# A recurrent attention layer with a sign-weight feed-forward part on one core: signs loaded in eight parts and the last block's loads in text order, two sums of products made by transfers, and zeros multiplied ahead of the first input

## The chip, the cores and the metric

The kernel runs on one core of a Trainium2 chip. A core has engines that run beside each other and meet through semaphores: PE (TensorE, matrix products; its weight loads, PEld, overlap the products), DVE (VectorE), ACT (ScalarE), POOL (GpSimd) and SP (SyncE). [...] Each engine takes its instructions in order.

The metric is the device time of one execution, in microseconds (us). Before the change it is 1445.28 us, the median of three runs (1454.41, 1443.0 and 1445.28).

## The reference

One layer over 2048 tokens of width 512, in float32. `_causal_dwconv` is a convolution of each channel over four tokens; `_lag(u, s)` is u moved by s tokens.

```python
xn = _layernorm(x)
# attention part: 16 heads of 128 channels, four lags
q = _silu(xn @ Wq); k = _silu(xn @ Wk); v = _silu(xn @ Wv); z = xn @ Wz
a = xn @ Wa; b = xn @ Wb
q, k, v = [_causal_dwconv(u, w) for u, w in ...]
q = q * cos + rot_half(q) * sin          # k the same way
q = q / max(norm(q), 1e-12)              # k the same way
for s in range(4):
    attn = einsum('bshd,bshd->bsh', q, _lag(k, s)) * scale
    gate = _sigmoid(_lag(a, s) * b)
    out = out + (attn * gate)[..., None] * _lag(v, s)
out = out * rsqrt(mean(out * out) + eps) * norm_w * _silu(z)
s = out @ Wout
# feed-forward part, with the signs of the weights
hidden = relu((xn @ sign(up_weight).T) * up_scale)
g = _silu((hidden @ sign(down_weight).T) * down_scale * output_scale)
result = x + s * g
```

## The kernel before

The 2048 tokens go in four blocks of 512 (b = 0 to 3), the 16 heads in eight pairs (p = 0 to 7), 256 channels each. Activations lie with channels on the 128 partitions and tokens along the free axis; `xnT` is the normalised input in this form. Products of float32 operands take two passes on PE, so a 128x512 product with four 128-row slices of weights shows up as eight PE instructions; a projection of one pair (two halves) is 16.

All PE and DVE instructions go through a small wrapper, `InOrder` (lines 68 to 78), which pins them to the order of the program's text. That is why the profile gives line 76 for nearly all of them; one tells them apart by tile. Instructions of ACT, POOL and SP are not wrapped: a scheduler places them, and their queues then run strictly in the order that it chose. A transfer that waits for a free buffer therefore holds up everything behind it on its queue.

*The start.* `first_layer_norm` (from line 144) loads the first 512 tokens in four chunks, takes their statistics on DVE and normalises them in place. `transpose` (168) turns each chunk on PE into a PSUM tile `tp`, which ACT copies into `xnT`. Then the first projection, `pq`, can start.

*The stage ahead of the blocks* (the loop with `step(p, -1, ...)`). For block 0 it makes q and k of each pair: projection, SiLU on ACT, convolution on DVE (`convolve`), rotation (`turn`), and in `products` (324) the products of q with the four lags of k, in two halves of 128 channels: tiles `pr` and `pr1`, 128x2048 each. The two are added; in block 0 DVE does that (line 361), in the other blocks, for even p, POOL issues an accumulating transfer (line 359). `sum_dots` later sums over the channels of a head by products on PE (`dots`). Beside this, the stage makes the feed-forward part of block 0 and writes the signs of the up and down weights to DRAM (`signs_dram`). Near its end, `gate_products(1)` sends four slices of gate products to DRAM: a plain transfer (227) and three accumulating ones (229), each of which waits for the one before it. They are on POOL's queue.

*The main loop.* For b = 0 to 2, `step(p, b)` makes v, the lag sums and the output of block b, and q, k of block b + 1. At p = 0 the sums of the block are turned into coefficients (`norms`, `norms_in_rows`, `coefficients`), which go to DRAM as `co_dram` and come back spread over partitions as `bc` (line 490): two tiles per pair, two transfers each, three buffers. `weighted` multiplies them with the lags of v (tiles `te`, `o`) on DVE; `gated_output` makes `oz`; `output_projection` (tile `po`) runs for two pairs at a time, and its results are added up in DRAM.

*The last block* has a loop of its own (line 736 on), with p one ahead of the output. It projects v (`pv`, weights `wv`) and z (`pz`, weights `wz`), all weights of v and z sharing three buffers with the tag `w` (`load`, line 246). Into memory that the first part no longer needs, POOL loads the signs of the up weights, `up` (4 MB), in four parts at p = 0 to 3, and `first_down` (1 MB) at p = 4. The loads of v are issued one p ahead. `raw`, `v`, `z` and `o` have one buffer each there.

*The feed-forward part of blocks 1 to 3* is a stream of up and down products on PE (`ph`, `pf`), with the hidden tiles of f split into two terms on DVE (`hid_hi`, `hid_lo`). In the last block the down products of the last four f are kept back and made by column chunk (0 and 1, then 2, then 3), so that DVE can finish one chunk (scale, SiLU on ACT, times y, plus x) while PE makes the next:

```python
if b == last and f >= NFC - 2:
    continue
_, df, terms = hids.pop(0)
```

The loop over f runs to NFC + 1, two past the last up product, and each turn takes one hidden tile, so this condition keeps four back.

Of the kernel before, what the change touches and what calls it, by code (L numbers as in the profile page):

```python
# [38 lines left out]
F32 = mybir.dt.float32  # L39
F32R = mybir.dt.float32r  # L40
AF = mybir.ActivationFunctionType
ALU = mybir.AluOpType
PSUM = bass.MemoryType.PSUM

P = 128
# [5 lines left out]
HALO = LAGS - 1  # L51
CH = H * D
KC = HID // P
NP = H // 2
TB = 512
# [5 lines left out]
NFC = FF // P  # L61
# [20 lines left out]
def recurrent_layer(ctx: ExitStack, tc: tile.TileContext, a: dict, out: bass.AP):  # L82
    nc = tc.nc
    pe, dve = InOrder(tc, nc.tensor), InOrder(tc, nc.vector)

    const = ctx.enter_context(tc.tile_pool(name="const", bufs=1))
    xnT = const.tile([P, KC, HALO + S], F32, name="xnT")
    ss_acc = const.tile([P, NT], F32, name="ss_acc")
# [76 lines left out]
        normalise(TC - 1)  # L165
        return x_in

    def transpose(x_in):
        for c in range(TC):
            tp = mm.tile([P, KC, P], F32, tag="mm", name=f"tp{c}")  # L170
            for k in range(KC):
                pe.transpose(tp[:, k, :], x_in[:, c, k * P : (k + 1) * P], ident)
            nc.scalar.copy(xnT[:, :, HALO + c * P : HALO + (c + 1) * P], tp)  # L173

    means = {}
# [68 lines left out]
    weights = {}  # L244

    def load(pool, n, p, b):
        w = pool.tile([P, KC, 2 * P], F32, tag="w", name=f"w{n}{p}_{b}", bufs=3)
        nc.sync.dma_start(w, a[f"w{n}"][p])
        weights[n] = w

    def with_halo(pool, name, tag, bufs, p, b):
# [22 lines left out]
    def raw_of(pool, n, p, b, bufs=2):  # L274

        raw = with_halo(pool, f"r{n}", "raw", bufs, p, b)
        project(n, p, b, raw[:, :, HALO:])
        keep_halo(f"r{n}", raw, p, b)
        return raw
# [44 lines left out]
    def products(p, b, q, between=None, beside_k=None):  # L324

        n = f"_{p}_{b}"
        load(qks, "k", p, b)
        q0 = q[:, LAGS - 1]
        k = with_halo(qks, "k", "k", 1, p, b)
        raw = raw_of(qks, "k", p, b)  # L330
        if p % 2 == 0:
            sum_squares()
        convolve(1, p, raw, k[:, :, HALO:])
        keep_halo("k", k, p, b)
        if between:
            between()
        turn(q)
        if beside_k:
            beside_k()

        sq = [qks.tile([P, 2, TB], F32, tag=f"sq{j}", name=f"sq{j}" + n, bufs=2 - j) for j in range(2)]
        for j in range(2):
            nc.scalar.activation(sq[j][:, 0], q0[:, j], AF.Square)
            nc.scalar.activation(sq[j][:, 1], k[:, j, HALO:], AF.Square)
        nc.gpsimd.dma_start(sq[0], sq[1], accum_op=ALU.add)
        squares_due.append((p, sq[0]))
        def product(to, j, lo, hi):

            k0 = k[:, j, lo : lo + TB]
            k_lags = bass.AP(k0.tensor, k0.offset, [k0.ap[0], [1, hi - lo], k0.ap[1]])  # L350
            dve.tensor_tensor(to, q[:, lo:hi, j, :], k_lags, ALU.mult)

        pr = qks.tile([P, LAGS, TB], F32, tag="pr", name="pr0" + n, bufs=2)
        product(pr, 0, 0, LAGS)
        if not b or p % 2 == 0:
            pr1 = qks.tile([P, LAGS, TB], F32, tag="pr", name="pr1" + n, bufs=2)
            product(pr1, 1, 0, LAGS)
            if b:
                nc.gpsimd.dma_start(pr, pr1, accum_op=ALU.add)
            else:  # L360
                dve.tensor_tensor(pr, pr, pr1, ALU.add)
        else:
            for lo in range(0, LAGS, 2):
                half = qks.tile([P, 2, TB], F32, tag="half", name=f"half{lo}" + n, bufs=1)
                product(half, 1, lo, lo + 2)
                dve.tensor_tensor(pr[:, lo : lo + 2], pr[:, lo : lo + 2], half, ALU.add)
        if not b:
            dots_due.append([p, pr, of_head[:, p], p == NP - 1, True])
            return


        for h in range(0, P, D // 2):
            first, second = slice(h, h + D // 4), slice(h + D // 4, h + D // 2)
            if p % 2 == 0:
                nc.gpsimd.dma_start(pr[first], pr[second], accum_op=ALU.add)
            else:
                both = dots_due[-1][1]
                nc.gpsimd.dma_start(both[second], pr[first])
                nc.gpsimd.dma_start(both[second], pr[second], accum_op=ALU.add)
        if p % 2 == 0:  # L380
            dots_due.append([p, pr, of_heads[:, p // 2], p == NP - 2, False])
        else:
            dots_due[-1][-1] = True
# [35 lines left out]
    squares = {}  # L419
# [40 lines left out]
    def values(p, b, raw):  # L460

        v = with_halo(vs, "v", "v", 1, p, b)
        convolve(2, p, raw, v[:, :, HALO:])
        keep_halo("v", v, p, b)
        return v
# [14 lines left out]
    def weighted(p, b, v):  # L480

        n = f"_{p}_{b}"
        o = vs.tile([P, 2, TB], F32, tag="o", name="o" + n, bufs=1)
        for s in range(LAGS):
            if s % 2 == 0:

                bc = vs.tile([P, 2, TB], F32, tag="bc", name=f"bc{s}" + n, bufs=3)
                for h in range(2):
                    row = co_dram[b][s : s + 2, 2 * p + h, :]
                    nc.sync.dma_start(  # L490
                        bc[h * D // 2 : (h + 1) * D // 2], row.partition_broadcast(D // 2)
                    )
            b2 = bc[:, s % 2].unsqueeze(1).to_broadcast([P, 2, TB])
            v_s = v[:, :, HALO - s : HALO - s + TB]
            if s == 0:
                dve.tensor_tensor(o, v_s, b2, ALU.mult)
            else:
                te = vs.tile([P, 2, TB], F32, tag="te", name=f"te{s}" + n, bufs=2)
                dve.tensor_tensor(te, v_s, b2, ALU.mult)
                dve.tensor_tensor(o, o, te, ALU.add)  # L500

        if p == 0:
            squares[b] = vs.tile([P, 2, TB], F32, tag="ss", name=f"ss{b}", bufs=1)
            nc.scalar.activation(squares[b], o, AF.Square)
        else:
            o2 = vs.tile([P, 2, TB], F32, tag="o2", name="o2" + n, bufs=1)
            nc.scalar.activation(o2, o, AF.Square)
            nc.gpsimd.dma_start(squares[b], o2, accum_op=ALU.add)
        return o

    def gated_output(p, b, o, z, wo):
# [47 lines left out]
    def step(p, b, beside_q=None, beside_k=None):  # L559
# [41 lines left out]
        if b + 2 < NTB:  # L601
# [4 lines left out]
            elif p == 5:  # L606
                divide(b + 2)

    x_in = first_layer_norm()
    small_loads()  # L610
    transpose(x_in)
    def in_two_terms(pool, x, tag, bufs, shape, name):
        hi = pool.tile(shape, F32R, tag=f"{tag}_hi", name=f"{name}_hi", bufs=bufs)
        lo = pool.tile(shape, F32R, tag=f"{tag}_lo", name=f"{name}_lo", bufs=bufs)
        dve.tensor_copy(hi, x)
        dve.tensor_tensor(lo, x, hi, ALU.subtract)
        return hi, lo
# [4 lines left out]
    def up_projection(ph, pool, f, b, up_f, xs):  # L622
        for k in range(KC):
            for i, term in enumerate(xs):
                pe.matmul(
                    ph,
                    up_f[:, k, :],
                    term[:, k, :],
                    start=(k == 0 and i == 0),
                    stop=(k == KC - 1 and i == 1),  # L630
                )
        hid = pool.tile([P, TB], F32, tag="hid", name=f"hid{f}_{b}", bufs=3)
        nc.scalar.activation(hid, ph, AF.Relu, scale=up_scale[:, f : f + 1])  # L633
        return in_two_terms(pool, hid, "hid", 4, [P, TB], f"hid{f}_{b}")


    G = 4
# [65 lines left out]
            step(p, b)  # L703

    last = NTB - 1
    load(vs, "v", 0, last)
    raw = raw_of(vs, "v", 0, last, 1)
    load(vs, "v", 1, last)
# [14 lines left out]
    NFD = 4  # L723
# [9 lines left out]
        return up[:, f].rearrange("p (k m) -> p k m", k=KC)  # L733


    for p in range(NP + 1):
        if 1 < p < NP:
            raw = raw_of(vs, "v", p, last, 1)
        if p:
            z, wo = gates_of_output(p - 1, last, zs)  # L740
        if p % 2 == 1:
            output_projections()
        if p < NP - 1 and p != 1:
            load(vs, "v", max(p + 1, 2), last)
        if 0 < p < NP:
            zs = weights_of_output(p, last)
            v = values(p, last, raw)
        if p:
            gated_output(p - 1, last, o, z, wo)
        if p < NP:  # L750
            o = weighted(p, last, v)
        if p < NFC // G:
            some = slice(G * p, G * p + G)
            nc.gpsimd.dma_start(up[:, some], signs_dram["up"][:, some])
        elif p == NFC // G:
            nc.gpsimd.dma_start(first_down, signs_dram["down"][:, 0:NFD])
        if p == 4:
            xs = in_two_terms(ffw, tokens(1), "xs", 1, [P, KC, TB], "xs1")
    hids = []
# [10 lines left out]
    with tc.tile_pool(name="ff", bufs=1, side="right") as ff, tc.tile_pool(  # L770
# [48 lines left out]
        for b in range(1, NTB):  # L819
            pf = [pfs.tile([P, HID], F32, name=f"pf{c}") for c in range(TC)]  # L820
            for f in range(2, NFC + 2):
# [13 lines left out]
                if f == NFC - 4 and b + 1 < NTB:  # L835
                    ahead = in_two_terms(
                        ff if b == 1 else ffw, tokens(b + 1), "xs", 1, [P, KC, TB], f"xs{b + 1}"
                    )
                if b == last and f >= NFC - 2:
                    continue  # L840
                _, df, terms = hids.pop(0)
                for c in range(TC):
# [87 lines left out]
```

## Time and profile before

The profile is of one execution, which took 1442.18 us, 1440.4 us of it the span between its first and its last instruction. The granted clock of PE was 0.99 on the mean.

| engine | busy, us | share of the span | instructions |
|---|---|---|---|
| PE (products) | 1401.4 | 97% | 3936 |
| PEld (weight loads) | 685.1 | 48% | 3936 |
| DVE | 1211.9 | 84% | 1363 |
| ACT | 612.9 | 43% | 1181 |
| POOL | 228.8 | 16% | 313 |

| transfers | packets | MB | share of 16 engines |
|---|---|---|---|
| issued by POOL (software queue) | 32512 | 104.89 | 38.0% |
| issued by SP (hardware queue) | 68624 | 153.53 | 36.4% |

The stages, by time from the start of the span: input and transposes until 11 us, the stage ahead of the blocks until about 210, the blocks 0 to 2 until about 1080, the last block until about 1256, the feed-forward part of the other blocks to the end. In a row of groups, waits or the timeline, "<-" between tiles reads "made from", and what stands after an idle time is who ended it. Lines such as L245 or L490 are lines of the kernel before; L76 is the wrapper.

### The profile page before, as it was taken

The numbers are of one execution on the slowest core, as the hardware profiler recorded it, in microseconds if no ns is written. First come the engines' busy times: TensorE is split into PE (matmuls) and PEld (weight loads), VectorE is DVE, ScalarE is ACT, GpSimd is POOL, SyncE is SP. The second block draws the span as 40 slices with busy tenths as digits, with TensorE's granted clock in tenths as the row PEclk, the third lists the DMA queues.
The fourth block names the chain that finished last, engine by engine and source line by source line (L and its number), as shares of the span: only waits on it lengthen the run. The fifth ranks groups of instructions, "written<-read, shape, count | busy, mean of one in ns | idle before, by whom it ended". The sixth has DMA issues, their size and how long they took to land.

```text
span 1440.4 us, 12555 instructions
## 1 busy us (share of the span) xinstructions
PE 1401.4 (97%) x3936; PEld 685.1 (48%) x3936; DVE 1211.9 (84%) x1363; ACT 612.9 (43%) x1181; POOL 228.8 (16%) x313
## 2 busy tenths in 40 slices
PE   7999999899999999999999999999996999999997
PEld 4555544344444444444444444444442444478886
DVE  6999998999999979999999899999893997146454
ACT  6565546345444544454444444444331333232122
POOL 2222121011212121112122211121211110200000
PEclk9999999999999999999999999999998999999999
DMA  9869676987998687879985898796769776562120
GB/s 339 258 166 203 158 200 156 220 213 179 186 228 194 137 193 229 197 184 200 210 197 139 182 216 212 179 210 146 161 142 273 209 188 143 82 232 89 30 88 29
DMA packets 101201, 259.20 MB, mean 180 GB/s; under 512 B 18768, under 2 KB 19280, under 8 KB 96272
## 3 DMA queue, kind: packets, MB, share of 16 engines
q0 software_dynamic: 32512, 104.89, 38.0%
q1 hardware_dynamic: 68624, 153.53, 36.4%
q8 instruction: 31, 0.51, 0.1%
q14 instruction: 34, 0.28, 0.1%
HBM read 157.67 MB, written 35.68 MB: 134 GB/s over the span
## 4 chain that ended last, share of the span: by engine, by line
PE 65%; DVE 21%; issue 6%; DMA 4%; ACT 2%; SPq 1%; POOL 0%; DVEq 0%; POOLq 0%; ACTq 0%
PE po L76 11%; PE pq L76 10%; PE pz L76 10%; PE pk L76 9%; PE pv L76 8%; PE ph L76 7%; PE pf L76 7%; DVE q L76 4%; DVE o L76 3%; DVE v L76 3%; DVE te L76 3%; DVE k L76 2%; DVE pr L76 2%; DMA wv<-in_wv_dram 1%; DVE oz L76 1%
## 5 line engine op out<-in xcount | busy, mean ns | idle before, releaser
L76 PE MATMUL pv<-xnT,wv 128*128 128x512 f32 x512 | 228.2, 598 | 15.7 <-DMA wv<-in_wv_dram 15.7
L76 PE MATMUL po<-wo,oz 128*128 128x512 f32 x512 | 227.1, 600 | 6.2 <-DVE oz L76 6.2
L76 PE MATMUL pq<-xnT,wq 128*128 128x512 f32 x512 | 228.4, 599 | 0.7 <-ACT xnT L173 0.7
L76 PE MATMUL pz<-xnT,wz 128*128 128x512 f32 x512 | 225.4, 592 | 0.0
L76 PE MATMUL pk<-xnT,wk 128*128 128x512 f32 x512 | 225.2, 592 | 0.0
L76 PEld LDWEIGHTS pv<-xnT,wv 128*128 128x128 f32 x512 | 96.3, 190 | 144.8 <-issue 119.6
L76 PEld LDWEIGHTS po<-wo,oz 128*128 128x128 f32 x512 | 97.0, 192 | 135.1 <-issue 109.7
L76 DVE SCALAR_TENSOR_TENSOR q<-rq,conv_w,q 128x512 f32<-128x512 f32 x192 | 141.4, 749 | 22.4 <-ACT q L284 17.9
L76 DVE SCALAR_TENSOR_TENSOR k<-rk,conv_w,k 128x512 f32<-128x512 f32 x192 | 142.0, 751 | 19.3 <-ACT k L284 14.7
L76 PEld LDWEIGHTS pq<-xnT,wq 128*128 128x128 f32 x512 | 96.9, 191 | 128.0 <-issue 119.9
L76 PEld LDWEIGHTS pz<-xnT,wz 128*128 128x128 f32 x512 | 96.4, 189 | 124.5 <-issue 121.3
L76 PEld LDWEIGHTS pk<-xnT,wk 128*128 128x128 f32 x512 | 96.6, 189 | 121.0 <-issue 117.6
L76 DVE SCALAR_TENSOR_TENSOR v<-rv,conv_w,v 128x512 f32<-128x512 f32 x192 | 141.4, 750 | 11.7 <-ACT v L284 7.2
L76 DVE SCALAR_TENSOR_TENSOR q<-q,turns 128x1024 f32<-128x1024 f32 (+1 forms) x128 | 127.1, 1014 | 4.0 <-ACT q L312 1.8
L76 DVE TENSOR_TENSOR te<-v,bc 128x1024 f32<-128x1024 f32 x96 | 117.0, 1218 | 4.5 <-DMA bc<-co_dram 4.5
L76 DVE TENSOR_TENSOR o<-o,te 128x1024 f32<-128x1024 f32 x96 | 117.6, 1225 | 3.3
L76 DVE TENSOR_TENSOR pr<-q,k 128x2048 f32<-128x2048 f32 x52 | 117.3, 2287 | 0.9
L633 ACT ACTIVATE hid<-ph,up_scale 128x512 f32<-128x512 f32 x64 | 43.8, 685 | 121.8 <-PE ph L76 121.1
L76 DVE CAST hid_hi<-hid 128x512 fp32r<-128x512 f32 x64 | 27.1, 424 | 73.8 <-ACT hid L633 73.8
L76 PE MATMUL ph<-xs_hi,up 128*128 128x512 f32 x192 | 76.4, 398 | 0.7 <-ACT so_sb L415 0.7
L76 PE MATMUL ph<-xs_lo,up 128*128 128x512 f32 x192 | 75.8, 395 | 0.0
L272 ACT ACTIVATE rq<-pq 128x512 f32<-128x512 f32 x64 | 38.1, 596 | 83.5 <-PE pq L76 83.3
(139 smaller groups left out, 1650.1 us busy)
## 6 DMA issues: line engine op xcount, KB each, us to landing
bc<-co_dram SPq DMA_DIRECT2D x128, 256.0 KB, 6.4
pr<-pr POOLq DMA_DIRECT2D x72, 256.0 KB, 6.0
wq<-in_wq_dram SPq DMA_DIRECT2D x32, 512.0 KB, 6.4
wk<-in_wk_dram SPq DMA_DIRECT2D x32, 512.0 KB, 5.7
sq<-sq POOLq DMA_DIRECT2D x32, 512.0 KB, 5.7
wv<-in_wv_dram SPq DMA_DIRECT2D x32, 512.0 KB, 5.3
wz<-in_wz_dram SPq DMA_DIRECT2D x32, 512.0 KB, 4.7
wo<-in_wo_dram SPq DMA_DIRECT2D x32, 512.0 KB, 6.4
```

Of the source, the lines that this page charges most:

```text
L76: return self.tc.keep_in_program_order(getattr(self.engine, op)(*args, **kwargs))
L272: nc.scalar.activation(to[:, j, :], pp, AF.Silu)
L633: nc.scalar.activation(hid, ph, AF.Relu, scale=up_scale[:, f : f + 1])
```

## The change

The diff, cut to its parts:

```diff
+    pool = InOrder(tc, nc.gpsimd)
+    loads = {"by": nc.sync}
...
-    def transpose(x_in):
+    def transpose(x_in, idle_work):
         for c in range(TC):
             tp = mm.tile([P, KC, P], F32, tag="mm", name=f"tp{c}")
             for k in range(KC):
                 pe.transpose(tp[:, k, :], x_in[:, c, k * P : (k + 1) * P], ident)
+            idle_work(TB // 2)
             nc.scalar.copy(xnT[:, :, HALO + c * P : HALO + (c + 1) * P], tp)
...
-        nc.sync.dma_start(w, a[f"w{n}"][p])
+        loads["by"].dma_start(w, a[f"w{n}"][p])
...
-            if b:
+            if b or p >= NP - 2:
                 nc.gpsimd.dma_start(pr, pr1, accum_op=ALU.add)
             else:
                 dve.tensor_tensor(pr, pr, pr1, ALU.add)
...
-                    nc.sync.dma_start(
+                    loads["by"].dma_start(
                         bc[h * D // 2 : (h + 1) * D // 2], row.partition_broadcast(D // 2)
                     )
...
-            nc.gpsimd.dma_start(squares[b], o2, accum_op=ALU.add)
+            pool.dma_start(squares[b], o2, accum_op=ALU.add)
...
+    still = qks.tile([P, 2, HALO + TB], F32, tag="raw", name="still", bufs=2)
+    nc.vector.memset(still[:, 0, :], 0.0)
+    unread = mm.tile([P, TB], F32, tag="mm", name="unread")
+
+    def idle_work(n):
+        pe.matmul(unread[:, 0:n], still[:, 0, 0:P], still[:, 0, 0:n], start=True, stop=True)
+
+    for n in (TB, TB, TB // 2):
+        idle_work(n)
     x_in = first_layer_norm()
...
-        return in_two_terms(pool, hid, "hid", 4, [P, TB], f"hid{f}_{b}")
+        return in_two_terms(pool, hid, "hid", 5, [P, TB], f"hid{f}_{b}")
...
     last = NTB - 1
+    loads["by"] = InOrder(tc, nc.sync)
...
+    v_weights = {}
     for p in range(NP + 1):
         if 1 < p < NP:
+            weights["v"] = v_weights.pop(p)
             raw = raw_of(vs, "v", p, last, 1)
...
-        if p < NP - 1 and p != 1:
-            load(vs, "v", max(p + 1, 2), last)
         if 0 < p < NP:
             zs = weights_of_output(p, last)
             v = values(p, last, raw)
+        if p + 2 < NP:
+            load(vs, "v", p + 2, last)
+            v_weights[p + 2] = weights["v"]
         if p:
             gated_output(p - 1, last, o, z, wo)
         if p < NP:
             o = weighted(p, last, v)
-        if p < NFC // G:
-            some = slice(G * p, G * p + G)
-            nc.gpsimd.dma_start(up[:, some], signs_dram["up"][:, some])
-        elif p == NFC // G:
-            nc.gpsimd.dma_start(first_down, signs_dram["down"][:, 0:NFD])
+        if p < NP:
+            some = slice(2 * p, 2 * p + 2)
+            pool.dma_start(up[:, some], signs_dram["up"][:, some])
+        else:
+            pool.dma_start(first_down, signs_dram["down"][:, 0:NFD])
...
-                if b == last and f >= NFC - 2:
+                if b == last and f >= NFC - 3:
                     continue
```

Five things change. In the last block, the loads of `wv`, `wz` and `bc` are pinned to the order of the text, and `wv` is asked for two p ahead, after the other loads of its turn. The up signs come in eight parts of 512 KB, one per p, each pinned behind the sum of squares (`ss`) of its p; `first_down` follows at p = 8. In block 0, the two halves of the products of the pairs 6 and 7 are added by a transfer that POOL issues. At the start, PE multiplies a tile of zeros into a bank that nothing reads: 1280 columns before x is there, and 256 after the transposes of each chunk. And five hidden tiles in place of four are kept back at the end, with a fifth buffer for them.

In the built program, the queues of POOL and SP stand as follows around the change. POOL: the transfer for pair 7 comes after the three accumulating `ab_dram` transfers of `gate_products(1)`, the one for pair 6 before the last two `f_dram` transfers of that stage. SP, last block: `co_dram`, `wv` (2), four `bc` (0), `wz` (1), `wv` (3), four `bc` (1), `wz` (2), `wv` (4), four `bc` (2), and so on; the `wo` loads are not pinned.

More of the change, by code (lines that the diff above doesn't have):

```diff
@@ L607, in step @@
                 divide(b + 2)
+    still = qks.tile([P, 2, HALO + TB], F32, tag="raw", name="still", bufs=2)
[5 more added lines that the diff above has]
+        idle_work(n)
     x_in = first_layer_norm()
     small_loads()
-    transpose(x_in)
+    transpose(x_in, idle_work)
     def in_two_terms(pool, x, tag, bufs, shape, name):
```

## The prediction

> **What bounds the kernel now.** I read the page first: PE is busy 97% of the span, and the chain of work that ended last runs 65% over PE lines, so time is to be had only where PE stands still or runs slowly. The waits of PE (what waited, for whom; total, times, longest, in us) give three places:
>
> ```profile
> PE pv L76 <- DMA wv<-in_wv_dram: 15.7, 1, 15.7
> PE tp L76 <- DVE x_in L76: 6.6, 3, 6.0
> PE po L76 <- DVE oz L76: 6.2, 3, 5.3
> ```
>
> A long wait costs more than itself. The table by windows (busy us and instructions of PE, PEld, DVE, ACT, POOL, then the granted clock, the DMA share, GB/s) shows half the clock after one:
>
> ```profile
> 283.00:287.00 4.00, 2.36 (x3) 1.17 (x4) 3.86 (x7) 3.80 (x5) 0.90 (x1) 0.50 1.06 211
> 287.00:291.00 4.00, 4.00 (x8) 1.62 (x7) 3.86 (x6) 1.11 (x2) 0.58 (x1) 0.70 1.10 210
> ```
>
> The timeline (start, duration, engine, line, operation, count, idle before) has both sides of the waits:
>
> ```profile
> 11.40 9.57 PE L76 MATMUL pq<-xnT,wq 128*128 128x512 f32 x16 [0.68 <-ACT xnT L173]
> ...
> 214.27 0.77 POOL L229 DMA_DIRECT2D ab_dram<-ab_sb  x1 [5.28 <-DMA ab_dram<-ab_sb]
> 218.39 1.06 PE L76 MATMUL dots<-pr,of_head 128*32 128x512 f32 x8
> 284.64 14.63 PE L76 MATMUL po<-wo,oz 128*128 128x512 f32 x28 [5.33 <-DVE oz L76]
> ...
> 1087.80 15.55 SPq L490 DMA_DIRECT2D bc<-co_dram  x8
> 1099.74 1.22 DVE L76 TENSOR_TENSOR o<-v,bc 128x1024 f32<-128x1024 f32 x1 [16.18 <-DMA bc<-co_dram]
> 1103.40 0.59 SPq L248 DMA_DIRECT2D wv<-in_wv_dram  x1
> 1107.84 1.23 DVE L76 TENSOR_TENSOR te<-v,bc 128x1024 f32<-128x1024 f32 x1 [4.47 <-DMA bc<-co_dram]
> 1118.66 6.75 PE L76 MATMUL pv<-xnT,wv 128*128 128x512 f32 x11 [15.67 <-DMA wv<-in_wv_dram]
> 1131.41 1.41 DVE L76 SCALAR_TENSOR_TENSOR oz<-o,norm_w,z 128x512 f32<-128x512 f32 x2
> 1134.25 13.90 PE L76 MATMUL po<-wo,oz 128*128 128x512 f32 x32
> ...
> 1428.98 1.41 DVE L76 SCALAR_TENSOR_TENSOR g<-pf,out_scale,down_scale 128x512 f32<-128x512 f32 x2 [1.27 <-PE pf L76]
> 1436.70 0.69 DVE L76 TENSOR_TENSOR g<-g,x 128x512 f32<-128x512 f32 x1
> ```
>
> At full clock 16 f32 products take 6.87 us (0.429 each). So the 28 from 284.64 to 299.11 lost 14.47 - 12.02 = 2.45 us, the 16 from 1118.66 to 1127.39 lost 8.73 - 6.87 = 1.9, and the first 16 of all, 11.40 to 20.81, lost 2.5.
>
> The profiled execution took 1442.18 us (span 1440.4); the median of the three runs is 1445.28, 3.1 above it. I sum against 1442.2.
>
> **Last block: loads in text order, up signs in parts.** Now: SP issues eight `bc` transfers ahead of `wv` (p = 3). The fourth pair waits for a buffer until 1102, so `wv` is issued at 1103.4 and lands 15.1 later, among 4 MB of up signs and 1 MB of down signs that POOL issues from 1088.4 to 1091.7. The same crowd makes the first `bc` pair land at 1099.6, the second at 1107.7.
>
> After: `co_dram`, `wv` (p = 2), four `bc`, `wz` (1), `wv` (3), four `bc`, and so on; POOL issues 0.5 MB of up signs here and each further part behind the `ss` sum of its p, some 15 us apart. At the three earlier block changes, without up signs, the first pair landed 8.1 to 8.6 us after its first issue and the second 9.9 to 10.6. From the issue at 1087.8 that is 1096.2 and 1098. DVE thus starts 3.5 us earlier and does not wait the 4.47: 8.0 us. The rest of its chain up to `oz` (seven products, a convolution, `oz`, seven products, a convolution, `oz`: 1112.7 to 1132.8) keeps its 20.1 us: first `oz` half at 1124.2 in place of 1132.2.
>
> PE: `wv` (2), issued at 1084 with the 3.2 to 5.4 us of its other landings, is there at 1087 to 1089.5, needed at 1089.1. `wz` (1) lands about 1098, needed at 1096 to 1097: up to 1.6 us. `pv` (3) and `pz` (2) are then done at 1117 to 1118.5, four products of `po` at 1120, and PE waits for `oz` until 1124.2: about 4 us, a new wait in the old one's place, off which I take one cold restart (1.9 to 2.45; 2.2). `po` ends at 1124.2 + 12.0 + 2.2 = 1138.4 against 1148.15: **-9.7**. Bounds: without the cold restart and with `bc` at the 5.7 us of its first landing, -13; with the first pair as late as now, only the 4.47 and none of the clock, -4.5. I stay by the three transitions, the nearest rows.
>
> Queued behind the new waits: each `wv` (p + 2) waits for `pz` (p - 1), and `bc` (p) stands behind it, so DVE's products of p start at least some 5 us (a `bc` landing) after `pz` (p - 1); DVE needs 14.3 us per p and PE 20.6, and `po` comes a pair later, so that hides. If `bc` took over 20 us there, it wouldn't. The ninth POOL step, first_down, goes out near 1243 in place of 1092; its first reader is past 1255, its landing 8 to 9 us, as other 1 MB transfers take; the last part of up signs, just before it, is read near 1300. Nothing.
>
> **First block: sums by transfer at p = 6 and 7.** Two DVE additions of 2.29 us (186.1, 205.9) go; DVE runs without a break from 56 to 214 and ends that stretch in the 5.33 us stall at 284.64, worth 7.8 with its cold part. But the additions become 1 MB accumulating transfers; the twelve of this kind (L359) land 7.7 to 15.6 us after issue, median 9.2. That of p = 6 is issued at 186.2 and lands by 195.4, just when `dots` reads it: nothing. That of p = 7 stands on POOL's in-order queue behind three `ab_dram` accumulations, each of which waits for the one before; the last is issued at 214.27. So it goes out at 214.8, not 201.4, and lands, on queues that are half idle there, about 8.2 us later: 223.0. PE wants it for `dots` at 218.39 and stands 4.6 us, with `pz`, `pq`, `pk` queued behind; cold restart 2.4. PE then reaches `po` at 279.3 + 7.0 = 286.3 and DVE, held by the later `pk`, at about 286: the stall at 284 is gone, and 7.8 - 7.0 = **-0.8** remains. At 7.7 and 1.8: -1.9; at the median: +0.2; at 15.6: +6.6.
>
> **Head: zeros multiplied.** 1280 columns before x, 256 after each chunk's transposes. The memset of 515 columns goes by 1 ns per column (128x12 takes 0.07, 128x32 0.09): an estimate of 0.6 us, done at 1.6, while DVE waits for x until 3.5. Cold products are 0.85 us per instruction, so the five instructions' worth ends at 5.9, where the first transpose starts at 5.96. If the clock is up by then, `pq` starts at 11.25 (wq lands at 11.21) and runs at full clock: 20.81 becomes 18.1, **-2.7**. The 256 columns (0.43 us warm) fit into the 1.45 us between chunks. PE and DVE both move, since neither waits for loads in this stretch. `still` holds one of the two `raw` buffers and `unread` one of six banks until the last zero product; the halo copy that ACT made at 2.15 (0.19 us) goes behind the transposes, and its tile is read from 24 on: nothing.
>
> **Tail: five hidden tiles kept back, not four.** DVE works without a gap from 1428.98 to 1437.39; it starts when the first pair's products end. With ten products per column chunk in place of eight, these end 4 x 0.233 = 0.93 us earlier relative to PE's end; scale of chunk 3 then waits 0.25 for PE: **-0.7**, bounds 0 and -0.9.
>
> Sum: -9.7 - 0.8 - 2.7 - 0.7 = -13.9: 1428.3 on the profile's scale.
>
> **Rivals.**
> *The zeros do not help (30%).* Before 16 us PE was 80% occupied by transposes and products from 6 on, and still slow, so transposes seem not to bring the clock up. [...] That speaks against this part: the zeros warm the clock, four chunks of transposes with 0.43 in 1.45 us let it fall. If it falls before `pq`, the zero products between transposes cost 0.85 each: `pq` starts 0.2 to 2.3 us later, less what was gained: +0.2 to +1.1 in place of -2.7. Total -10.5, 1431.7. For the forecast: PE has no idle gap over 0.5 us there.
>
> *The last block is given back (14%).* `bc` comes as late as it does now, or `wz` late too: total about -8.5, 1433.7.
>
> *More than summed (17%).* The wait at `oz` stays short and warm, or p = 7's transfer lands sooner: -18, 1424.
>
> *Slower (3%).* One mechanism: p = 7's sum. It costs its landing time minus 3.6, plus 2.4 of clock, minus 7.8; the other parts (-13) are eaten from a landing of 22 us on, such as first_down's 22.8 in the crowd at 1092. The DMA share is 0.5 from 214 to 218, so there is no such crowd; slower by 1% would need 36.
>
> *The change does not do it (1%)*: the built order has the loads in text order.
>
> **Numbers.** Forecast 35%. 1% of the median is 14.4 us, about what a measurement tells from no change. On the scale of the median, a run like the profiled one stands up to 3.1 low; I add half: 1428.3 + 1.6, **1430**. Range: the part bounds together run from -20 to -7, and 0 to 3.1 for the scale: 1423 to 1438. Faster by over 1% (under 1430.8): about half of the forecast, all of the larger case and some of the first rival, 0.43; within 1%: 0.54; slower 0.03.
>
> **What would show it.** A PE wait at `dots` for DMA `pr`, 3 to 6 us near 215, and none at `po` near 280; `wv` absent from PE's waits, `po` waiting 2 to 6 us for `oz` near 1120; the first `bc` pair landing 8 to 9 us after issue; `pq` at 6.9 us for 16 products; DVE's tail start 0.9 earlier against PE's end. The forecast is wrong if `pq` still takes 9 us, or if `bc` lands later than 11 us.

## The result and the profile after

The changed kernel takes 1438.91 us, the median of 16 runs (1433.76 to 1443.7), beside 1443.89 us for the kernel before in 16 runs: a ratio of 0.9959, 95% interval 0.9941 to 0.9976. That is 5.0 us less. 13.9 were forecast on the scale of the profile; 1430 lies under all 16 runs, and the median stands 0.9 us above the range of 1423 to 1438. The profiled execution took 1443.7 us (span 1441.9), the slowest of the 16, 1.5 us more than the profiled one of before. (In one later comparison, that of `e16_wo_again`, one disturbed execution, the profiled one, is left out; no number below is read from it.)

The waits of PE (what waited, for whom; total, times, longest, in us) have changed places:

```profile
PE po L76 <- DVE oz L76: 9.4, 5, 7.7
PE dots L76 <- DMA pr<-pr: 7.6, 2, 4.3
PE dots L76 <- issue: 3.2, 1, 3.2
PE pv L76 <- DMA wv<-in_wv_dram: 2.2, 1, 2.2
```

The wait of 15.7 for `wv` is down to 2.2 and the one of 6.6 for x is nearly gone. But `po` waits longer than before, and `dots`, which hardly waited, stands three times. The timeline (start, duration, engine, line, operation, count, idle before and who ended it) has the places:

```profile
11.53 7.14 PE L76 MATMUL pq<-xnT,wq 128*128 128x512 f32 x16 [0.24 <-ACT xnT L177]
221.40 1.93 PE L76 MATMUL dots<-pr,of_head 128*32 128x512 f32 x8 [4.29 <-DMA pr<-pr]
426.31 1.93 PE L76 MATMUL dots<-pr,of_heads 128*32 128x512 f32 x8 [3.34 <-DMA pr<-pr]
718.55 1.07 PE L76 MATMUL dots<-pr,of_heads 128*32 128x512 f32 x8 [3.15 <-issue]
1096.80 7.11 PE L76 MATMUL pv<-xnT,wv 128*128 128x512 f32 x16 [2.23 <-DMA wv<-in_wv_dram]
1127.62 12.28 PE L76 MATMUL po<-wo,oz 128*128 128x512 f32 x28 [0.50 <-DVE oz L76]
1242.33 15.36 PE L76 MATMUL po<-wo,oz 128*128 128x512 f32 x28 [7.70 <-DVE oz L76]
```

Compare the starts of the same work in both profiles; that gives a running account. After the head PE is 2.3 us ahead (`pk` at 18.51 against 20.81), at 138 still 1.4, at `pz` past the first block's stall 3.5 (295.60 against 299.11). At the two later waits for `dots` the lead goes and turns into a lag of 5.3 (735.04 against 729.73). The last block wins 13.6 of its own (`pv` at 1139.74 against 1147.99) and then loses 11.0 in one place: `so` starts at 1257.62 against 1254.83. From there to the end it wins 1.3, of which 0.7 is the tail's.

The one place is the last line above: 7.7 us without work, and then 28 products in 15.4 us where the same 28 took 12.3 at 1127. The table by windows (busy us and instructions of PE, PEld, DVE, ACT, POOL, then granted clock, DMA share, GB/s) shows why they are slow:

```profile
1236.00:1240.00 4.00, 0.00 (x0) 0.00 (x0) 3.97 (x4) 0.00 (x0) 0.00 (x0) 0.79 0.00 0
1240.00:1244.00 4.00, 1.67 (x2) 0.84 (x3) 3.83 (x7) 1.06 (x1) 1.19 (x3) 0.50 0.00 0
1244.00:1248.00 4.00, 4.00 (x6) 1.69 (x5) 1.03 (x3) 0.58 (x1) 1.86 (x3) 0.50 0.98 192
```

From 1236 to 1244 DVE is busy and no transfer moves: DVE makes the products of p = 7 that it should have made long before. DVE's own rows say how long it stood:

```profile
1150.94 1.23 DVE L76 TENSOR_TENSOR o<-v,bc 128x1024 f32<-128x1024 f32 x1 [8.41 <-ACT z L276]
1192.71 1.23 DVE L76 TENSOR_TENSOR o<-v,bc 128x1024 f32<-128x1024 f32 x1 [9.79 <-DMA bc<-co_dram]
1233.01 1.23 DVE L76 TENSOR_TENSOR o<-v,bc 128x1024 f32<-128x1024 f32 x1 [11.79 <-DMA bc<-co_dram]
```

These are the first products of p = 3, 5 and 7, and each waits for its `bc`. (The first row names ACT, whose `z` came just before; the second of the two `bc` transfers that the product reads was issued at 1139.8 and landed 11.1 us later, at 1150.9.) SP's queue shows what stood ahead of these `bc`:

```profile
1138.22 0.33 SPq L474 DMA_DIRECT2D wo<-in_wo_dram  x1
1138.60 0.42 SPq L76 DMA_DIRECT2D wv<-in_wv_dram  x1
1139.11 3.26 SPq L76 DMA_DIRECT2D bc<-co_dram  x4
...
1179.42 0.33 SPq L474 DMA_DIRECT2D wo<-in_wo_dram  x1
1179.81 0.49 SPq L76 DMA_DIRECT2D wv<-in_wv_dram  x1
1180.39 2.65 SPq L76 DMA_DIRECT2D bc<-co_dram  x4
...
1220.63 0.33 SPq L474 DMA_DIRECT2D wo<-in_wo_dram  x1
1221.38 2.58 SPq L76 DMA_DIRECT2D bc<-co_dram  x4
```

`wo` goes out 1.5 us ahead of the end of an output projection each time (1139.7, 1181.0, 1222.2): it has three buffers, and at odd p the next comes free only when the output products have read it. `wv` and `bc` follow within 1 us; they had been standing behind it. In the kernel before, the last two `bc` transfers of p = 7 went out 22 us ahead of that `wo`:

```profile
1206.93 1.23 SPq L490 DMA_DIRECT2D bc<-co_dram  x2
1228.88 0.33 SPq L470 DMA_DIRECT2D wo<-in_wo_dram  x1
```

### The profile page after: what moved, and what is told of

Read it like the earlier page. It is cut to its first block, busy times and chain, and to the rows that moved or that the text cites. A ratio compares the mean times of both kernels' runs of the same rounds, so it can differ in the third digit from the quotient of the medians.

```text
span 1441.9 us, 12588 instructions
## 1 busy us (share of the span) xinstructions
PE 1408.2 (98%) x3950; PEld 686.5 (48%) x3950; DVE 1207.8 (84%) x1362; ACT 611.4 (42%) x1181; POOL 232.4 (16%) x319
## 5 line engine op out<-in xcount | busy, mean ns | idle before, releaser
L76 PE MATMUL po<-wo,oz 128*128 128x512 f32 x512 | 230.5, 607 | 9.4 <-DVE oz L76 9.4
```

The costliest lines, as they stand in the source:

```text
L76: return self.tc.keep_in_program_order(getattr(self.engine, op)(*args, **kwargs))
```

## The experiments

They ran in five groups, each on a chip of its own, beside the kernel before: e1 to e4, e5 to e8, e9 to e12, e13 to e15, e16 to e18. The median of the kernel before was 1444.6, 1452.8, 1453.2, 1450.8 and 1450.1 us in them, so ratios are compared, and best those of one group.

**e1: wo behind bc.** The changed kernel with the load of `wo` moved in the text behind `weighted`, and pinned.

```diff
-            zs = weights_of_output(p, last)
+            load(vs, "z", p, last)
+            wz = weights["z"]
             v = values(p, last, raw)
...
             o = weighted(p, last, v)
+            if p:
+                zs = wz, load_wo(p, last)
```

> The changed kernel, with the load of wo of each p of the last block pinned behind the bc of its p; it stands ahead of them in the built order of the changed kernel, and at odd p it waits for the end of the output products that free its buffer. Theory (wo holds up bc): bc of p = 3, 5 and 7 is issued 12 to 15 us earlier against the output products, DVE's three waits of 8 to 12 us for bc fall below 4 us, PE's wait of 7.7 us at po near 1235 falls below 1 us and its 28 products take 12.0 us in place of 15.4: about 10.8 us less, 1428 (1425 to 1432). Rival (wv, which waits for the last product of z, holds up bc as well): bc comes as late as before, 1438 to 1440. Rival (DVE is behind for another reason): bc earlier, but po still waits over 4 us, 1433 to 1440.

Measured: 1430.53 us, ratio 0.9903 (0.9875 to 0.9932). The longest wait at `po` is 1.7 us, and near 1232 there is none. SP's queue in this profile:

```profile
1117.45 7.30 SPq L76 DMA_DIRECT2D bc<-co_dram  x4
1131.03 0.33 SPq L76 DMA_DIRECT2D wo<-in_wo_dram  x1
...
1188.43 4.47 SPq L76 DMA_DIRECT2D bc<-co_dram  x4
1213.44 0.33 SPq L76 DMA_DIRECT2D wo<-in_wo_dram  x1
```

`wo` waits as long as ever, with nothing urgent behind it. The `bc` of p = 7 goes out 25 us ahead of it. `wv` was not what held `bc` up.

**e2, e3, e4, e5: one part alone.** The kernel before with only the last block's part (order and parts of the up signs), only the zeros, only the two sums, only the tail.

> Only the last block's part of the change (loads in text order, up signs in eight parts). Theory (it gains some 14 us before 1150 and gives some 11 back behind 1230): no wait for wv over 3 us, three waits of DVE for bc of 8 to 12 us, a wait at po of 7 to 8 us near 1238, ratio 0.996 to 0.999 (1 to 5 us less than the kernel before). As the prediction had it (nothing given back): ratio 0.993, 1434.

Measured: 1.0002 (0.9985 to 1.0018), a little worse than the theory. The waits are as it said: `wv` 2.2, `po` 7.4 at 1240. In this profile the last block is 12.7 us ahead of the kernel before at `pv` near 1138 and gives 10.2 of that back by its end; in the medians nothing is left.

> Only the zeros ahead of the first input. Theory: the first projections run at full clock, pk starts 2.3 us earlier (18.5 against 20.8), and most of it is lost again where PE waits for transfers or for DVE (at po near 285 and at dots near 427 and 715), which do not move as much: 0 to 1.5 us less at the end, ratio 0.999 to 1.000. Rival (PE alone sets the end, so a gain at the head stays): 2.3 us less, ratio 0.9984.

Measured: 0.9987 (0.9965 to 1.0009), which doesn't tell the two apart. In its profile the lead of 2.6 at `pk` is still 2.7 at 712, so there it was not lost.

> Only the transfers that add the products of the pairs 6 and 7 of the first block. Theory: a wait of 3.5 to 5 us at dots near 218, PE's wait at po near 285 gone, PE 1.5 to 2.5 us earlier at 300; then up to 2 us are lost at dots near 427, since the transfers read there do not come earlier: between 2 us less and 1 us more at the end, ratio 0.9985 to 1.0007. Rival (the wait at dots outweighs the other): 3 or more us slower, ratio over 1.002.

Measured: 1.0022 (1.0003 to 1.0040), slower, nearer to the rival. The wait at `dots` is there (4.0), but the one at `po` is only halved (2.8, at 288), and PE is 3.2 us later at 300. DVE did not keep what the two additions freed:

```profile
224.36 3.35 DVE L76 RECIPROCAL r<-r 64x512 f32<-64x512 f32 x1 [3.27 <-ACT r L435]
...
242.09 0.69 DVE L76 SCALAR_TENSOR_TENSOR rk<-dots,rk 128x512 f32<-128x512 f32 x1 [4.73 <-DMA rk<-r]
```

It waits for the norms, and then for the transfers that spread them over rows (`rk<-r`). In the whole change the second of these waits is missing, and the stall at 285 with it. Why the two differ was not tried.

> Only the tail's part of the change (five hidden tiles kept back in place of four). Theory: DVE's run of scale, gate and sum at the end starts 0.9 us earlier against the last product, 0.5 to 1.3 us less, ratio 0.9992 to 0.9996, which this many runs can hardly tell from none. Rival (no gain, the last products set the end anyway): ratio 1.000.

Measured: 1.0006 (0.9981 to 1.0031), which can't be told from none, as expected.

**e6 and e7: the sums ahead of ab_dram.** e6 pins POOL's order so; e7 adds e1's edit and puts `wv` (2) ahead of `co_dram`.

```diff
-                nc.gpsimd.dma_start(pr, pr1, accum_op=ALU.add)
+                (nc.gpsimd if b else pool).dma_start(pr, pr1, accum_op=ALU.add)
...
+        by = pool if b == 1 else nc.gpsimd
-        nc.gpsimd.dma_start(to, ab[0:LW, :])
+        by.dma_start(to, ab[0:LW, :])
```

> The changed kernel with one thing more: POOL's order is pinned so that the transfers that add the products of the pairs 6 and 7 go out ahead of the four ab_dram transfers. Theory (the wait of 4.3 us at dots near 218 is the place of pair 7's transfer in POOL's queue): it is issued at about 202 instead of 213.1 and lands by 212; the wait at dots near 218 and the slow clock behind it (2.4) are gone, part of it comes back as a wait of up to 3 us at po near 283; 3 to 6 us less than the changed kernel, 1433 to 1436, ratio 0.992 to 0.995. Rival (the transfer itself, not its place, is late): still a wait over 2 us at dots near 218, no gain, 1438 to 1439. Rival (what is won here is lost again at dots near 425 and 715): the wait near 218 is gone and the time stays within 1.5 us of 1439.

> The changed kernel with three loads put elsewhere: wo behind the bc of its p in the last block, wv of p = 2 ahead of co_dram, and the sums of the pairs 6 and 7 ahead of ab_dram. Theory (the three places are separate): 8.4 (wo, as measured) plus 3 to 6 (sums) plus 0.5 to 2.5 (wv) less than the changed kernel's 1438.9: 1422 to 1427, ratio 0.985 to 0.988. Rival (they share a wait further on): 1428 to 1431.

Measured: e6 0.9968 (0.9948 to 0.9988), e7 0.9917 (0.9885 to 0.9949). Neither ratio is better than that of the kernel it was made from (0.9959 and 0.9903). The wait near 218 is gone in both; in e6 waits of 4.3 at `dots` (279.86) and 4.9 at `po` (290.20) come in its place. POOL, ACT and DVE in e6:

```profile
217.83 0.77 POOL L76 DMA_DIRECT2D ab_dram<-ab_sb  x1 [11.15 <-DMA ab_dram<-ab_sb]
221.93 0.76 POOL L76 DMA_DIRECT2D ab_dram<-ab_sb  x1 [3.34 <-DMA ab_dram<-ab_sb]
...
224.65 0.77 POOL L76 DMA_DIRECT2D ab_dram<-ab_sb  x1 [1.03 <-DMA ab_dram<-ab_sb]
```

```profile
228.63 0.58 ACT L433 COPY sq<-squares 64x512 f32<-64x512 f32 x1 [8.89 <-DMA ab_dram<-ab_sb]
```

```profile
229.25 0.68 DVE L76 TENSOR_TENSOR r<-sq,squares 64x512 f32<-64x512 f32 x1 [9.70 <-ACT sq L433]
```

The norms need that `sq`, a copy that ACT writes into the buffer of `ab_sb`: both have the tag `rk`, which has one buffer. The last transfer of the chain reads it until it lands, 3.9 us after 224.65. In the changed kernel that transfer is issued at 212.57, and the same copy runs at 215.63. So it is the chain of four transfers, each waiting for the one before, that costs, and whoever waits for its end pays: pair 7's transfer behind it on POOL's queue (4.3 us of PE at `dots` in the changed kernel), or the norms, which want its buffer (8.9 us of ACT here).

**e8: no zeros among the transposes.** The line `idle_work(TB // 2)` is taken out; the zeros ahead of x stay.

> The changed kernel without the 256 columns of zeros after each chunk's transposes; the 1280 columns ahead of x stay. Theory (transposes do not hold the clock): it rises near 6 us and falls again before or just after the first projection begins, and the 16 products of pq take 8 to 9.6 us as in the kernel before. Rival (what the zeros ahead of x won holds through the transposes): the 16 products take 6.9 us and the fill was not needed.

One execution (1455.93 us, against a median of 1452.83 before):

```profile
10.64 7.14 PE L76 MATMUL pq<-xnT,wq 128*128 128x512 f32 x16 [0.68 <-ACT xnT L176]
```

The rival held here: full clock without the fill (16 products in 7.14 us, as in the changed kernel), and `pq` 0.9 earlier. But `e15_combined`, without the fill as well, has this (windows):

```profile
6.00:8.00 2.00, 1.27 (x9) 0.84 (x8) 1.93 (x5) 0.49 (x2) 0.00 (x0) 1.00 0.71 147
8.00:10.00 2.00, 1.21 (x8) 0.84 (x7) 1.41 (x6) 1.66 (x6) 0.00 (x0) 0.82 1.01 379
10.00:12.00 2.00, 1.32 (x5) 0.79 (x4) 0.65 (x1) 0.94 (x2) 0.00 (x0) 0.50 0.89 314
```

PE is busy for 62% of 6 to 10, nearly all of it transposes, and the granted clock falls from 1.00 to 0.82 and then 0.50; `pq` then takes 9.5 us. In all twelve profiles with the fill that are read here, `pk` starts 2.1 to 2.8 us earlier than before the change. So the gain came twelve times out of twelve with the fill and once in two without it. e15 is as the theory had it; e8, with its 7.14 us, shows that the clock does not fall in every execution. In e8 the first transposes were also slower (the first eight took 2.12 us, the next eight 1.31; in e15 the first four took 0.63), and no run separates the part of the transposes from that of the 38% in which PE stood still in e15.

**e9 and e10, on top of e1.** e9 makes the `dots` of p = 6 in the blocks 0 to 2 after the output products, in place of ahead of them. e10 makes only pair 6's sum by a transfer.

```diff
-        if due and not change:
+        later = due and not change and p == NP - 2
+        if due and not change and not later:
             sum_dots()
...
         output_projections(sum_dots if change else None)
+        if later:
+            sum_dots()
```

> The kernel with wo behind bc, and in the blocks 0 to 2 the dots of p = 6 made after the output products instead of ahead of them. Theory (PE's waits at dots near 426 and 715, 0 to 4.4 us and a slow clock behind the longer ones, differ from run to run and take back part of what is won earlier): both waits gone, the time 1 to 5 us under that of the kernel with wo behind bc alone, ratio 0.987 to 0.9897. Rival (the output products then wait for DVE's oz instead): a new wait at po near 423 and 712, ratio 0.990 to 0.992.

> The kernel with wo behind bc, with the sum of pair 6 alone made by a transfer, that of pair 7 by DVE as before the change. Theory (pair 7's transfer costs 4.3 us at dots near 218 and 2.3 of clock, and what it saves DVE is partly lost in the wait for the norms): no wait at dots near 218, a wait of 2 to 3.5 us at po near 284 without a slow clock behind it, PE 2 to 4 us earlier at 300 than with both transfers; ratio 0.987 to 0.989. Rival (half the relief leaves the stall near 284 long enough for a slow clock): 5 us and more lost there, ratio 0.990 to 0.993.

Measured: e9 0.9797 (0.9764 to 0.9830), e10 0.9826 (0.9797 to 0.9856), but the kernel before was 9 us slower in this group than in e1's, so neither is compared with e1 by this. e9's waits at `dots` near 426 and 715 are gone. e10's wait at `po` near 284 was 3.4 us, and the 28 products behind it took 13.7 where 12.0 is full clock, between theory and rival; `pz` behind them starts at 297.3, no earlier than in e1 (296.8). One sum or two makes no difference that these runs show.

**e11 and e12: the order without the parts, the parts without the order.** e11 is e1 with the up signs as before the change. e12 is the kernel before with only the eight parts:

```diff
-        if p < NFC // G:
-            some = slice(G * p, G * p + G)
-            nc.gpsimd.dma_start(up[:, some], signs_dram["up"][:, some])
+        if p < NP:
+            some = slice(2 * p, 2 * p + 2)
+            pool.dma_start(up[:, some], signs_dram["up"][:, some])
```

> The kernel with wo behind bc, but the up signs loaded in four parts of 1 MB without pinning, as before the change. Theory (the order removes the wait for wv, the parts bring bc sooner): no wait over 3 us for wv; the first bc pairs land as late as before the change, some 8 us later than with eight parts, and PE waits 5 to 9 us for oz at po near 1120 with a slow clock behind it; ratio 0.994 to 0.997. Rival (the order alone does it): no such wait, ratio 0.989 to 0.992.

> The kernel before, with one thing changed: the up signs in eight parts, each behind the ss sum of its p, first_down at p = 8. Theory (the parts alone shorten the wait for wv, since bc lands sooner, frees its buffer sooner and so lets wv out sooner, but wv still stands behind bc): wait for wv 4 to 9 us in place of 15.7, ratio 0.994 to 0.998. Rival (only the order counts): wait for wv 12 us or more, ratio 0.999 to 1.001.

Measured: e11 0.9905 (0.9875 to 0.9935), e12 0.9868 (0.9839 to 0.9898). e12, one part alone, on the old order, is better than the whole change, by ratio (0.9959) and by median (1435.27 against 1438.91). It beat its own theory; in its profile

```profile
1091.81 9.77 SPq L491 DMA_DIRECT2D bc<-co_dram  x8
1101.63 0.59 SPq L249 DMA_DIRECT2D wv<-in_wv_dram  x1
```

`wv` still stands behind eight `bc`, but the transfers are quick enough now: the wait for `wv` is 3.3 us. e11 has the order, and the crowd of 5 MB as before: `wz` (1) lands 14.3 us after its issue at 1095.67, PE waits 4.3 us for it until 1110, and its 16 products take 9.6. Without the parts the order moves the wait; it was not at `po`, as I had it.

**e13, e14, e15.** e13 is the changed kernel with only the order taken back (the loop's loads as before the change, `loads["by"]` left at `nc.sync`); e14 is the changed kernel again; e15 is e13 with e9's edit and without the fill.

> The changed kernel without the pinned order: the loads of wv, wz and bc of the last block stand where they stood before the change (wv one p ahead); the eight parts of the up signs, the sums, the zeros and the tail stay. Theory (the order, which puts wo ahead of bc, is what gives the last block's gain back): no wait over 2 us at po near 1240, a wait for wv of 2 to 5 us near 1105, 9 to 15 us less than the changed kernel on the same chip. Rival (the order is worth as much as it costs, and the rest of what is missing lies in the waits at dots): within 3 us of the changed kernel.

> The changed kernel as it is, beside the one with its order undone. Theory: a wait of 7 to 9 us at po near 1240 again, and at dots near 426 and 715 waits of another length than in its first profile (3.3 and 3.2 us); ratio 0.994 to 0.998. Rival (the wait at po near 1240 was of that one execution): no such wait, ratio under 0.99.

> The kernel with the order undone, with the dots of p = 6 made after the output products, and without the zeros among the transposes. Theory (the parts add up once nothing takes them back): 3 to 8 us under the kernel with the order undone, ratio 0.972 to 0.982. Rival (a wait at po for oz, or for wv, takes it back): within 2 us of the kernel with the order undone.

Measured in one group: e13 1434.98 us, 0.9885 (0.9853 to 0.9917); e14 1443.95, 0.9958 (0.9936 to 0.9979); e15 1431.65, 0.9876 (0.9848 to 0.9905). Taking the order back is worth 9.0 us. The last output products of the block, in e13 and then in e14:

```profile
1235.83 13.89 PE L76 MATMUL po<-wo,oz 128*128 128x512 f32 x32
```

```profile
1242.65 14.04 PE L76 MATMUL po<-wo,oz 128*128 128x512 f32 x28 [7.72 <-DVE oz L76]
```

The waits at `dots` near 426 and 715 add up to nearly the same in both: 1.5 and 2.6 in e13, 2.3 and 1.9 in e14. e15 is 3.3 us better than e13, though its profile has the slow `pq` and a wait of 5.3 for `wv`.

**e16, e17, e18: is it the dots?** e16 is e1 again, e17 is e9 again, e18 is e13 with e9's edit.

> The kernel with wo behind bc once more, as the base for the two beside it on one chip. Theory: no wait over 2 us at po near 1232; waits of 0 to 5 us at dots near 426 and 715; ratio 0.985 to 0.991.

> The kernel with wo behind bc and the dots of p = 6 after the output products, beside the one without that move. Theory (the waits at dots near 426 and 715 take back part of what is won before them): 3 to 7 us under the kernel beside it. Rival (the gain seen before was of the chip): within 1.5 us of it.

> The kernel with the order undone and the dots of p = 6 after the output products, with the zeros among the transposes kept. Theory (wo behind bc in the pinned order is worth 1 to 3 us more than no pinned order, since wv comes in time): 0 to 3 us over the kernel with wo behind bc and the dots moved; pq's 16 products at 6.9 us each time, where without the zeros among the transposes one execution had 9.5. Rival (no order is better): under it.

Measured in one group: e16 0.9857 (0.9829 to 0.9885), e17 1424.54 us, 0.9817 (0.9788 to 0.9847), e18 1425.40 us, 0.9825 (0.9801 to 0.9849). 0.9857 of the 1450.09 before is 1429.4, so the move of the `dots` gives 4.9 us, though the intervals overlap. In e17

```profile
422.85 13.90 PE L76 MATMUL po<-wo,oz 128*128 128x512 f32 x32
436.68 1.07 PE L76 MATMUL dots<-pr,of_heads 128*32 128x512 f32 x8
```

PE waits at neither: `oz` is there, and the sums have 14 us more to land. e17 and e18 differ by less than a microsecond, so in the whole time the pinned order, with `wo` put right, is worth nothing that these runs show. e17 beats both kernels, by 1.8% and some 1.4% (against e14's ratio).

**The last block by itself.** One stretch of each profile leaves out all that lies before the last block, the waits at `dots` too: from the start of one row of `so` products (1081.13 in the profile of before) to that of the next (1254.83).

| loads of the last block | profiles | us |
|---|---|---|
| as before the change | before, e3, e4, e5 | 173.7 to 177.0 |
| order with `wo` ahead, eight parts (the change) | after, e2, e6, e8, e14 | 169.4 to 175.0 |
| order with `wo` behind, four parts of 1 MB | e11 | 167.3 |
| no order, eight parts | e12, e13, e15, e18 | 161.5 to 164.0 |
| order with `wo` behind, eight parts | e1, e7, e9, e10, e17 | 158.0 to 160.5 |

The parts alone win some 12 us of it. The order alone, with `wo` behind `bc`, wins 6.4 or more in its one profile. On top of the parts it adds some 3 with `wo` behind, which the whole times don't show, and takes back 5 or more with `wo` ahead.

## Why the prediction was wrong

Point by point.

- **Last block: the step that failed.** The prediction listed what is queued behind the new waits, and named only `wv` waiting for `pz`; it said that this hides, since `po` comes a pair later. `wo` is in that queue too, unpinned, and the front of this document says so. It waits for `po` itself, 12 to 13 us longer than `wv` does (at p = 3 the last `pz` that `wv` waits for ends at 1125.2, `wo` goes out at 1138.2; at p = 5 1167.2 and 1179.4). The prediction had even the point from which it would show ("if `bc` took over 20 us there"), but not the transfer that does it. Shown three ways: moving `wo` alone (e1, 8.4 us under the changed kernel, by medians from two groups in which the kernel before agrees within 0.7), taking the order back (e13 against e14, 9.0 us in one group), and the last block alone (e2, nothing gained). The table of the last block says the same. The missing part of the forecast, 13.9 - 5.0 = 8.9, is of this size.
- **Last block, first half: right in kind, too small.** 9.7 forecast, 13.6 measured. `wv` (2) was issued 5.7 us before PE wanted it (1088.87 against 1094.57), much as forecast (1084 against 1089.1), but it landed after 7.8 us, and PE waited 2.2 for it. The 3.2 to 5.4 us of its other landings left out the slow ones: in the profile of before one more of the last block took 11.0, and in the blocks ahead of it they took up to 15.4. The first `bc` pair, though, was there 5.2 us after its issue (1094.00 to 1099.22), not 8.4, and so `po` waited 0.5 us and not 4, and no cold restart followed (its 28 products took 12.3 us). The rows of the earlier block changes were the wrong neighbours; the first landing of 5.7 us, which I kept as a bound, was the right one.
- **Who earned it.** I gave the gain to order and parts together. e12 and e11 show that it is mostly the parts: with them the transfers came sooner on either order. On the old one the eight `bc` went out in 9.8 us in e12 and 15.6 before, and `wv` was there 6.9 us after its issue (1101.63 to 1108.55), before 15.1. On the new one `wz` (1) landed after 7.8 us in the changed kernel and 14.3 in e11. The order alone, with `wo` put right, wins less (167.3 us for the last block, where the parts alone make it 161.5 to 164.0).
- **Sums of pairs 6 and 7.** The place in POOL's queue behind `ab_dram` was right, and so was its size: 4.6 forecast, 4.3 measured. In the ten other profiles with both sums in that place it is 3.1 to 5.2. The net was -0.8 forecast and -2.1 in this profile (138 to 299), but +2.5 us by medians in e4 alone. The step "the stall at 284 is gone" held in this profile (0.3 us) and not in e4 (2.8), where DVE stood 4.7 us for `rk` first; why it did is open.
- **Head.** -2.7 forecast, -2.3 measured. The likeliest rival, that zeros don't help, fell. What it feared did happen once without the fill (e15, 9.48 us for the first 16 products); with it the first 16 products took 7.14 us in all twelve profiles.
- **Tail.** -0.7 forecast. DVE's scale starts 4.70 before PE's last product (1434.98) in place of 3.77 (1432.75), 0.93 earlier as forecast, and DVE's last row starts 3.27 after it in place of 3.95:

```profile
1430.28 1.41 DVE L76 SCALAR_TENSOR_TENSOR g<-pf,out_scale,down_scale 128x512 f32<-128x512 f32 x2 [2.20 <-PE pf L76]
...
1438.25 0.69 DVE L76 TENSOR_TENSOR g<-g,x 128x512 f32<-128x512 f32 x1
```

- **What the sum left out.** It took every term as if nothing lay between it and the end. `dots` at 427 and 715 lie between. In the profile of before the last transfer of the sums landed 2.3 us before PE asked for them at 427; at 715 it held PE for 0.8. With the lead of 3.4 us PE would have waited 1.1 at 427 for the same landing; it waited 3.3, since the sums also landed 2.1 later. At 715 PE was 1.3 behind already and still waited 3.2, since they landed 3.7 later. A slow clock goes with both waits (0.58 from 426 to 430, 0.69 from 718 to 722). Why the sums landed later is open. These waits differ from run to run (e1: 1.5 and 0.7; e4: 0.6 and 3.1; after: 3.3 and 3.2), and the kernel before can have them as well (e5, whose code is that of before there: 4.2 and 1.9; e2: 0 and 3.2). The prediction's base was a profile that happened to have almost none.

## What to carry to other kernels

When loads are pinned to an order, walk the whole in-order queue of that engine, the unpinned ones too, and ask of each which buffer it waits for and who reads that last: a load that isn't urgent, waiting on a late reader, must stand behind the urgent ones (`wo` ahead of them cost 7.7 us at `po` here). Ask the same of a chain of transfers: who waits behind it, and who wants its buffer. Try a large background load in parts that go out as the main work proceeds; that alone was worth more here than the order (161.5 to 164.0 us for the last block against 167.3), and it needs no knowledge of who comes first. Add up gains only as far as the next place where two chains meet with a microsecond or two to spare, and give such a place slack before counting what is won ahead of it.

## What was not expected of the hardware

The same transfers differed by some microseconds between executions: the three-step sum ahead of `dots` at 715 ended when PE had waited 0.7 us (e1) or 3.2 (after), with the same code. The median of the kernel before went from 1444 to 1453 us between the groups, each on another chip. And four chained transfers of 64 KB took from 195.38 to past 213 on POOL's queue, issued 4.7, 6.6 and 5.9 us apart, which made them dearer here to whoever stood behind them (17.7 us until pair 7's transfer went out at 213.10) than that transfer of 1 MB itself (8.3 us to its landing).
